# Storing the kept transposes of a two-layer banded kernel: the DMA issued by ScalarE in place of SyncE

## The chip, the cores and the metric

The kernel runs on one core of a Trainium2 chip. The core has a matrix engine (TensorE; PE in the profile, with its weight loads shown as PEld), a vector engine (VectorE, DVE), an activation engine (ScalarE, ACT), a general engine (GpSimd, POOL) and SyncE (SP), which here does nothing but issue DMAs. Each engine works through its own list of instructions in order and waits on semaphores for the others. The time is the device time of one execution in microseconds. An issue of a DMA stands in its engine's list like any other instruction; the transfer itself runs on 16 DMA engines.

## The reference

Two layers of the same form are applied to an image of 512 x 512 positions with 64 channels. In each, the input is normalised by groups of two channels over the whole image, then by channels at each position, and projected to 128 hidden channels five times (left, its gate, right, its gate, an output gate). The left values are read near the diagonal alone: output row i takes nine rows i-4 to i+4, each times one left value for the pair of rows and channel. The result is normalised over channels, gated, projected back and added to the input.

```
m, mask = src_mask, m[:, None] * m[None, :]
xn    = ln(group_norm(x))                          # 1 x 512 x 512 x 64
left  = (xn @ Wl + bl) * mask * sigmoid(xn @ Wlg + blg)
right = (xn @ Wr + br) * mask * sigmoid(xn @ Wrg + brg)
gate  = sigmoid(xn @ Wog + bog)
out[i, j, h] = sum over d in -4..4 of left[i+d, i, h] * right[i+d, j, h]
x     = x + (ln(out) * gate) @ Wo + bo             # and the same again with the second layer's weights
```

## The kernel before, in words

The rows are cut into nine overlapping blocks of 64 (`row_blocks`). The 128 partitions hold the 64 rows of a block twice: once for a column in the left half of the image and once for the column 256 further on. A chunk is 128 columns of each half, so there are 18 chunks a layer. A chunk is worked through in 16 units of eight columns (`Unit`, `NU`), 288 units a layer. One unit is one step of the loop in `layer` (line 846).

A unit passes these stages, several steps apart, so that in one step the engines work on different units:

- `load` (399) brings the unit's z from DRAM in two DMAs. GpSimd or VectorE applies the group norm (`scaled`, `moved`), VectorE takes statistics (`inner_stats`), GpSimd centres and rescales (`centred`, `rescaled`).
- `transposed` (452) turns z on TensorE into PSUM, and `kept` (471) copies the transposes to SBUF as the tile zT with ScalarE. zT has 192 columns for each of four column pairs: the first 128 are the transposes of both halves, written by a first activation of 128 x 512 elements; the last 64 repeat the first half, written by a second of 128 x 256. The pool `ztp` (1066) has two buffers for zT.
- zT serves `right` (516), eight products each for two halves of the unit, with `right_gate` (519, the sigmoid tile sg, on ScalarE) and `right_end` (523, the product into RO, on VectorE).
- The first 128 columns of zT are also stored in DRAM, in the tensor `later`, for the output gate, which is needed about 30 steps on (`LAG`, 787). `recall` (686) fetches them back as the tile zg two steps ahead of use; its pool `ztg` (1067) has two buffers. `gates` (690) projects zg on TensorE and `gated` (703) applies the sigmoid with ScalarE (the tile gate).
- `mix` (577) does the banded product with slabs A of the left values, which `take_left` (561) fetches from the DRAM tensor `left_of` in four DMAs each, eight slabs a chunk; ScalarE and VectorE copy the results back to RO ("copy a", "copy b").
- `norm` (675) writes the tile on, mostly by ScalarE, one or two of eight columns by GpSimd. `turned` (714) transposes it on TensorE, `times_gate` (727) makes ZH on VectorE, `end` (750) projects back, `ended` (763) adds the input (the tile XR, fetched by `fetch`, 739) and stores the output in two DMAs.

At the start of each layer some steps also make left values (`left`, 530), which are stored to `left_of` in groups of nine DMAs.

The order on each engine is written by hand. The lists `FIRST` and `SECOND` (38 to 54) name the stages of a step in order, for the first and the second layer; `InOrder` (373) keeps what is issued through `en` in the order of the program on its engine. A step starts with its DMAs (848 to 857): loads of z, the fetch of XR, slabs A, and zg. Then come the stages of the list; "keep" stands behind "transpose", and "end", with the output's stores, soon behind "keep". On ScalarE a step of the first layer runs, from "keep" on: two activations of zT, copies to RO, statistics in every fourth step, three of on, two of gate, two of sg, four of on.

A waiting instruction holds up all that stands behind it on its engine. All DMAs, whichever engine issues them, use eight semaphores in turn; each waits until the DMA eight places before it in the program's order has landed.

The helper that keeps the order records nearly every instruction at line 381, so the profile's rows are told apart by their tiles.

Of the kernel before, what the change touches and what calls it, by code (L numbers as in the profile page):

```python
# [16 lines left out]
P = 128  # L17
# [86 lines left out]
def tile_two_banded_layers(  # L104
# [366 lines left out]
    def kept(u: Unit):  # L471
        u.t = ztp.tile([P, JU // 2, P + S], F32, tag="zT", name="zT")
        to = u.t.rearrange("c k (n p) -> c n k p", n=3)
        for n, pt in enumerate(u.pt):
            en.scalar.activation(
                to[:, n : n + pt.shape[1]], pt.rearrange("c n (k p) -> c n k p", p=S),
                AF.Identity, bias=1.0,
            )
        if u.near is None:
            en.scalar.activation(  # L480
                to[:, 2], u.pt[0][:, 0].rearrange("c (k p) -> c k p", p=S), AF.Identity, bias=1.0
            )
            en.sync.dma_start(later[u.at], u.t[:, :, :P])

    def place(k: int, e: int) -> int:

# [297 lines left out]
    def layer(src: bass.AP, dst: bass.AP, w: dict, stats: bool, then=None):  # L784
# [61 lines left out]
        for t in range(min(loads), last_t + 3):  # L846
# [40 lines left out]
            for item in order:  # L887
# [41 lines left out]
                elif name == "keep":  # L929
                    for v in inputs(t + 1):  # L930
                        kept(v)
# [132 lines left out]
    later = dram.tile([len(blocks) * LH // JU, P, JU // 2, P], F32, name="later")  # L1064
# [45 lines left out]
```

## Time and profile before

| | |
|---|---|
| median of 3 runs | 4771.6 us (4764.16 to 4789.46) |
| the profiled execution | 4769.15 us |
| its span, first to last instruction | 4767.2 us |
| TensorE busy | 3885.2 us (81%) |
| weight loads busy | 3337.2 us (70%) |
| VectorE busy | 4007.1 us (84%) |
| ScalarE busy | 3608.6 us (76%) |
| GpSimd busy | 3274.7 us (69%) |
| granted TensorE clock, mean | 0.952 |
| DMA moved | 983.48 MB, 206 GB/s over the span |
| DMAs of `later` | 576 stores and 576 loads of 256 KB |

The busy shares are means over the whole span, of which about the first 270 us go to the statistics of the input and the setup, and a stretch near 2,450 to 2,650 us to the change from the first layer to the second. The layers' steady parts lie between. Issues of DMAs do not count as busy, so SyncE has no row in the table; its load is read from the rows of its issues (their queue is called SPq) and from its timeline. A wait's row says which engine waited before which tile, what ended the wait, the microseconds in total, how many times, and the longest.

### The profile page before, as it was taken

The page shows a single profiled execution, that of the slowest core. Times are in us where ns is not written, and L with a number is a line of the kernel's source. Part 1 is how long each engine was busy: PE and PEld are TensorE (multiplying, and loading weights), DVE is VectorE, ACT ScalarE, POOL GpSimd, SP SyncE. Part 2 cuts the span into 40 slices and gives each one's busy share as a digit, 9 for nine tenths or more (in the row PEclk, how much of TensorE's full clock was granted, in tenths as well). Part 3 has the DMA queues.
Part 4 walks back from the last instruction along what each step waited for, and adds up shares of the span by engine and source line. Part 5 has one row for each costly group of instructions (what it writes and reads, how often), then busy time and mean ns, then how long its engine had stood idle before and what let it go on. Part 6 is the DMA issues. An engine that isn't in the chain of part 4 may idle for free. (4 is left out here: it accounts for less than half of the span.)

```text
span 4767.2 us, 193179 instructions
## 1 busy us (share of the span) xinstructions
PE 3885.2 (81%) x76306; PEld 3337.2 (70%) x76306; DVE 4007.1 (84%) x10943; ACT 3608.6 (76%) x8410; POOL 3274.7 (69%) x3427
## 2 busy tenths in 40 slices
PE   1035899999999999999985478888888888888898
PEld 0024787888787878887864467777777777777776
DVE  7864888888888888888877488988899998999898
ACT  0023888888888888898974378888888888888887
POOL 0036888888888888888723487777777777777751
PEclk9987999999999999999997799999999999999999
DMA  7958677777777777777764867777777777777776
GB/s 311 401 120 126 182 208 204 212 217 211 212 208 208 210 208 209 214 212 210 207 171 110 104 189 208 214 220 208 210 221 214 221 212 211 213 219 215 217 200 185
DMA packets 1437809, 983.48 MB, mean 206 GB/s; under 512 B 167363, under 2 KB 1284585, under 8 KB 1432553
## 3 DMA queue, kind: packets, MB, share of 16 engines
q1 hardware_dynamic: 1432064, 969.69, 74.4%
q8 instruction: 604, 9.90, 0.9%
q14 instruction: 301, 2.46, 0.2%
q10 hardware_dynamic: 4840, 1.43, 0.1%
HBM read 658.35 MB, written 312.40 MB: 204 GB/s over the span
## 5 line engine op out<-in xcount | busy, mean ns | idle before, releaser
L381 ACT ACTIVATE on<-RO,nm,rs 128x128 f32<-128x128 f32 x3744 | 1588.5, 492 | 91.8 <-DVE nm L381 44.9
L381 PEld LDWEIGHTS banks<-pack,zT 64*128 64x128 f32 x18576 | 1304.4, 203 | 380.6 <-ACT zT L381 204.4
L381 PE MATMUL banks<-pack,zT 64*128 64x128 f32 x18576 | 1350.8, 292 | 174.4 <-ACT zT L381 149.3
L381 DVE TENSOR_TENSOR RO<-banks,sg 128x512 f32<-128x512 f32 (+1 forms) x1188 | 796.3, 677 | 464.4 <-ACT sg L381 387.6
L381 POOL TENSOR_SCALAR on<-RO,rs,nm 128x128 f32<-128x128 f32 x864 | 383.9, 451 | 975.7 <-ACT sg L381 504.5
L381 ACT ACTIVATE sg<-banks 128x512 f32<-128x512 f32 (+1 forms) x1188 | 695.0, 590 | 311.1 <-PE banks L381 287.1
L381 PE MATMUL bank<-zg,pack 64*128 64x448 f32 (+1 forms) x2304 | 727.3, 615 | 213.5 <-DMA zg<-later 193.8
L381 DVE BATCH_NORM_STATS2 sto<-RO 128x6 f32<-128x256 f32 x2304 | 803.8, 412 | 0.8
L381 DVE SCALAR_TENSOR_TENSOR ZH<-bank,pack,gate 128x448 f32<-128x448 f32 (+1 forms) x1152 | 739.5, 684 | 63.0 <-ACT gate L381 34.1
L381 ACT ACTIVATE gate<-bank 128x448 f32<-128x448 f32 (+1 forms) x1152 | 563.8, 541 | 172.6 <-issue 103.0
L381 POOL TENSOR_TENSOR z<-z,ga 128x512 f32<-128x512 f32 x536 | 681.2, 1279 | 17.2 <-DMA z<-mid_x 8.7
L381 PE MATMUL bank<-pack,ZH 128*64 128x64 f32 x18432 | 667.3, 226 | 17.8 <-DVE nm L381 16.7
L381 POOL TENSOR_TENSOR z<-z,gb 128x512 f32<-128x512 f32 x536 | 677.5, 1277 | 5.1
L381 POOL TENSOR_TENSOR z<-z,rs 128x512 f32<-128x512 f32 x586 | 618.3, 1056 | 71.6 <-DVE rs L381 44.6
L381 POOL TENSOR_TENSOR z<-z,sti 128x512 f32<-128x512 f32 x586 | 624.3, 1066 | 20.8 <-DVE sti L381 20.8
L381 PEld LDWEIGHTS bank<-pack,ZH 128*64 128x64 f32 x18432 | 587.4, 138 | 60.9 <-DVE nm L381 24.2
L381 ACT ACTIVATE zT<-banks 128x512 f32<-128x512 f32 (+1 forms) x1084 | 460.1, 475 | 72.0 <-PE banks L381 62.8
L381 DVE BATCH_NORM_STATS2 sti<-z 128x6 f32<-128x128 f32 x2344 | 504.1, 282 | 0.5 <-POOL z L381 0.3
L381 PE MATMUL bank<-ident,on 64*128 64x64 f32 x9216 | 453.8, 227 | 27.5 <-ACT gate L381 25.0
L381 PEld LDWEIGHTS bank<-zg,pack 64*128 64x128 f32 x2304 | 240.5, 191 | 336.5 <-DMA zg<-later 62.7
L381 PEld LDWEIGHTS bank<-ident,on 64*128 64x128 f32 x9216 | 426.5, 141 | 69.6 <-ACT gate L381 44.7
L381 DVE TENSOR_TENSOR XR<-bank,XR 120x512 f32<-120x512 f32 (+1 forms) x576 | 390.9, 679 | 2.5 <-PE bank L381 1.2
(154 smaller groups left out, 4020.5 us busy)
## 6 DMA issues: line engine op xcount, KB each, us to landing
later<-zT SPq DMA_DIRECT2D x576, 256.0 KB
A<-left_of SPq DMA_DIRECT2D x1152, 128.0 KB
zg<-later SPq DMA_DIRECT2D x576, 256.0 KB
z<-in_x_dram SPq DMA_DIRECT2D x576, 128.0 KB
z<-mid_x SPq DMA_DIRECT2D x576, 128.0 KB
gn_x<-in_x_dram SPq DMA_DIRECT2D x16, 4096.0 KB
XR<-in_x_dram SPq DMA_DIRECT2D x448, 112.0 KB
mid_x<-XR SPq DMA_DIRECT2D x448, 112.0 KB
```

Of the source, the lines that this page charges most:

```text
L381: return lambda *a, **k: tc.keep_in_program_order(f(*a, **k))
```

## The change

The store of a unit's transposes is issued by ScalarE; the data, the tiles and all else in the program stay.

```diff
     def kept(u: Unit):
         u.t = ztp.tile([P, JU // 2, P + S], F32, tag="zT", name="zT")
...
             en.scalar.activation(
                 to[:, 2], u.pt[0][:, 0].rearrange("c (k p) -> c k p", p=S), AF.Identity, bias=1.0
             )
-            en.sync.dma_start(later[u.at], u.t[:, :, :P])
+            en.scalar.dma_start(later[u.at], u.t[:, :, :P])
```

The store stays at its place in the program: directly behind the activations that write zT. On ScalarE the copies, on, gate and sg of the step now stand behind it; on SyncE the next DMA behind the fetch of zg is the store of the output.

## The prediction

> **What bounds the kernel now.** I read the windows first, to separate the two layers from their starts; then the waits; then SyncE's issues and its timeline beside ScalarE's. Busy time in two steady windows (columns: stretch, length, busy us and instructions per engine, granted clock, DMA share, GB/s):
>
> ```profile
> 700.00:2400.00 1700.00, 1583.57 (x32684) 1373.20 (x32677) 1466.60 (x3976) 1510.88 (x3537) 1396.24 (x1376) 0.98 0.76 210
> 2700.00:4600.00 1900.00, 1650.13 (x32720) 1439.55 (x32716) 1698.98 (x4623) 1558.24 (x3592) 1438.23 (x1586) 0.96 0.77 212
> ```
>
> Order: PE, PEld, DVE, ACT, POOL. In layer one PE is busy 93%, ACT 89%, DVE 86%; in layer two DVE 89%, PE 87%, ACT 82%. No compute engine is full, so something makes them wait for each other. The queue of DMA issues is not in these columns. Its rows (min/median/max ns):
>
> ```profile
> L381 SPq DMA_DIRECT2D later<-zT x576: 518/553/4745, 281.1 to 4622.3; - x192
> L381 SPq DMA_DIRECT2D A<-left_of x1152: 573/615/2165, 422.8 to 4666.2; - x192
> L381 SPq DMA_DIRECT2D zg<-later x576: 338/458/1883, 499.1 to 4755.4; - x192
> ```
>
> A step (one unit of eight column pairs; 288 a layer) issues on average one later, two A, one zg, two z (587), two XR in (462 or 481) and two XR out (480 or 506): 5.35 us by the medians, near 6.1 with 0.05 to 0.1 us between issues, and more with the tails. A step lasts 1700/231 = 7.4 us in layer one, 1900/268 = 7.1 in layer two, counting the evacuations zT in each window. SyncE is as full as PE, and its work comes in bursts. Its timeline (start, us, count) and what ScalarE and PE do meanwhile:
>
> ```profile
> 3000.49 1.06 SPq L381 DMA_DIRECT2D later<-zT  x1
> 3001.64 1.03 SPq L381 DMA_DIRECT2D out_dram<-XR  x2
> 3002.77 1.16 SPq L381 DMA_DIRECT2D z<-mid_x  x2
> 3003.99 1.02 SPq L381 DMA_DIRECT2D XR<-mid_x  x2
> 3005.11 3.62 SPq L381 DMA_DIRECT2D A<-left_of  x4
> 3008.83 0.55 SPq L381 DMA_DIRECT2D zg<-later  x1
> 3009.48 0.55 SPq L381 DMA_DIRECT2D later<-zT  x1
> ...
> 3014.08 0.56 SPq L381 DMA_DIRECT2D later<-zT  x1
> ```
> ```profile
> 3003.12 0.84 ACT L381 ACTIVATE zT<-banks 128x512 f32<-128x512 f32 x2
> 3003.86 0.89 ACT L381 ACTIVATE on<-RO,nm,rs 128x128 f32<-128x128 f32 x2
> ```
> ```profile
> 3012.12 1.87 PE L381 MATMUL bank<-zg,pack 64*128 64x448 f32 x4 [3.35 <-DMA zg<-later]
> ```
>
> From store to store SyncE needs 8.99 us in the step with A, 4.60 in the next without. The zT made at 3003.12 to 3003.96 is stored at 3009.48: SyncE is 5.5 us late. The zg issued at 3008.83 is read by PE at 3012.12, 3.29 us later, after PE idled 3.35. The waits in total (us, times, longest), the last two lines from the layer-one and the layer-two window:
>
> ```profile
> PE bank L381 <- DMA zg<-later: 193.8, 103, 6.9
> ACT zT L381 <- DMA later<-zT: 104.2, 13, 16.3
> SPq L381 <- ACT zT L381: 234.9, 122, 12.7
> DVE RO L381 <- ACT sg L381: 201.1, 267, 4.6
> DVE RO L381 <- ACT sg L381: 121.0, 83, 9.6
> ```
>
> So SyncE's lateness costs PE 194 us (zg) and ScalarE 104 us (a zT buffer still held by its late store). The second is at the starts of the layers, for instance:
>
> ```profile
> 341.81 14.34 SPq L381 DMA_DIRECT2D left_of<-RO  x9
> ...
> 366.91 0.66 ACT L381 ACTIVATE zT<-bank 128x256 f32<-128x256 f32 x2 [16.33 <-DMA later<-zT]
> ```
>
> **The change, part by part.** The built program moves 576 stores from SyncE to ScalarE, each behind the two activations that fill zT; PE, DVE and POOL keep their order, and no other DMA moves. Each store still waits for two things: the activation that fills the stored columns, and, as every DMA here does, the transfer eight places earlier in program order, whose semaphore it reuses.
>
> *Removed from SyncE.* One issue a step, 0.553 us by the median and some 0.1 between issues: 0.65 us a step, 11 steps of a burst giving back 7 us. The wait for zT goes too (234.9 us), but the stores of XR behind it wait for DVE at about the same place, so I count no gain for that. What was late next was zg. Its mean wait is 193.8/103 = 1.9 us, three stores' worth, so it should vanish from the third or fourth step of a burst on. I take two thirds: **-129 us**. Ends: 0 (SyncE stays late because a transfer, not the issue, sets it) and -194.
>
> *The held zT buffers.* At 341.81 nine stores of left_of keep SyncE for 14.34 us and zT's store waits behind them. From ScalarE it is issued without that queue, but its eighth predecessor is then often one of the nine, which must land. I take half of 104.2: **-50**; ends 0 and -104.
>
> *Added to ScalarE.* Without the store the instruction behind zT starts 0.74 us after zT's start (3003.12 to 3003.86). With it the first activation must end (0.58, the mean of 128x512 zT), then 0.04, the issue of 0.553, and 0.04 again (ScalarE's own issues at line 218 take 607 ns and start 648 apart): 1.21. The delay is 0.47; with the tail of the store's row (up to 4745 ns) I take 0.53, or 305 us for 576. The cover is ScalarE's idle time: (1700-1511)/231 = 0.82 us a step in layer one, (1900-1558)/268 = 1.27 in layer two. Behind the store in ScalarE's order stand the copies RO, the norms on, the two gates and the two sg; DVE's RO waits for sg, and frees banks for PE. sg ended a wait of DVE 267 times of 464 in the layer-one window and 83 of 542 in the layer-two window. So 0.53 x 288 x 0.58 = 88 us reach DVE in layer one and 0.53 x 288 x 0.15 = 23 in layer two. DVE is not the fullest engine of layer one and its RO is not always awaited; I take half: **+56**. Ends: 0 (ScalarE idle covers all) and +305 (cover gone).
>
> *The new wait.* ScalarE now waits at its store for a transfer that SyncE issues. No row shows this, so I take it from the step above: eight places before the store of 3009.48 stands the second z, issued about 3003.35, landing 3.29 us later, at 3006.6; zT ended at 3003.96, so ScalarE would have stood 2.6 us, with copies, gates and sg behind it. The freed 0.65 us a step shrinks the lateness, so I take one hold of 2 us in each of the 36 chunks (18 a layer, 16 steps each): **+72**. Ends: 0 (SyncE is never late) and 288 slab steps (1152/4) times 2.6, which is 749, if nothing shrinks and nothing covers.
>
> Sum on the profiled execution: 4767.2 - 129 - 50 + 56 + 72 = 4716, and 2 us outside the span (4769.15 against 4767.2) make **4718 us**. The profiled execution is 2 us under the median 4771.6, so no correction is needed.
>
> The Trainium skill speaks against this gain: in "DMA: Bandwidth & Descriptors", section "Issuing engines are not separate DMA queues", moving issues to another engine saves only the sequencer's time, usually small beside the transfer. Row: the issue is 0.55 us beside 3.29 to landing, small for one transfer, but ten a step fill SyncE. By the rule the sum is no change, 4769; by the rows it is 4718.
>
> The same page, section "Queues, rings and completion order", says that SyncE and ScalarE have no descriptor generator each of their own. In the trace, ScalarE's line-218 issues stay at 607 to 618 ns where one of SyncE's falls into them. If the rule meant that one waits out half of the other's issue, 0.27 us in 85% of 576 cases would be 132 us more on ScalarE.
>
> **The rivals.** (1) *ScalarE becomes the bound of layer one.* For it: 89% busy plus 0.53/7.4 is 96%. Against it: 0.82 us idle a step. Price: all of 0.53 x 288 = 153 there, 12 in layer two, no hold: 4769 - 129 - 50 + 165 = 4755, no change that a measurement tells (0.5%, 24 us). (2) *ScalarE is held by SyncE's transfers.* Place: its store in slab steps. For it: 5.5 us of lateness, where a step of this kind holds from about 2.8 on (6.1 us from the predecessor's issue to the store, less 3.29 to land). Against it: SyncE gains 0.65 us in each step. Price: 1.3 us (half of 2.6) in 288 steps, of which idle covers 0.8, is +144; zg gains only half (-65), and -50 and +56 stay: 4769 + 85 = 4854. It decides when SyncE's lateness in slab steps stays above 2.8 us. (3) *ScalarE's issue hides altogether and zg's wait ends:* 4769 - 194 - 50 + 28 = 4553. For it: idle time covers 0.53 in the mean step; against it: sg is awaited in most steps of layer one.
>
> **How the numbers follow.** Forecast 4718 (own range 4640 to 4745): 0.39; rival 3: 0.08; rival 1: 0.16; rival 2 and worse: 0.37. Faster by over 0.5% is 0.47, within it 0.16, slower 0.37. The range runs from 4630, between forecast and rival 3, to 4880, a little above rival 2: left out are about 0.08 below and 0.1 above.
>
> **What would show it.** PE's wait for zg well under 100 us; ScalarE's waits for later at the layer starts halved; ScalarE's gap behind zT near 0.5 us in most steps; waits of ScalarE's queue for z, XR or A in the hold, some 70 us. DVE's wait for sg should grow by under 100. Wrong would be: zg's wait unchanged (SyncE's issue was not the limit), ScalarE's store taking over 0.8 us, or holds of 2 us in most slab steps.

## The result, and the profile after

The changed kernel takes 4640.5 us (median of 4 runs, 4633.4 to 4643.1) against 4772.9 of the kernel before on the same chip: a ratio of 0.9729, 95% interval 0.9699 to 0.9759. The direction was forecast, with the time in the range; the size was not: 2.7% against the forecast 1.1%. The profiled execution has a span of 4641.2 us, 126.0 less than before; the sum of the prediction had 51 less.

The two windows of the changed kernel (second one 100 us shorter, since the kernel ends earlier; columns as before):

```profile
700.00:2400.00 1700.00, 1613.57 (x33373) 1384.28 (x33365) 1491.87 (x4038) 1529.45 (x3610) 1398.26 (x1382) 0.99 0.77 214
2700.00:4500.00 1800.00, 1632.40 (x32093) 1393.97 (x32093) 1674.88 (x4530) 1521.38 (x3570) 1388.06 (x1547) 0.98 0.80 219
```

In the first window each engine does more work in the same time: PE is busy 95% where it was 93%, DVE 88% (86%), ScalarE 90% (89%). In the second DVE has gone from 89 to 93%. The waits that the prediction spoke of, in the changed kernel's list (us, times, longest):

```profile
DVE RO L381 <- ACT sg L381: 248.3, 324, 4.3
...
PE bank L381 <- DMA zg<-later: 31.3, 21, 5.8
...
PEld bank L381 <- DMA zg<-later: 17.2, 13, 3.3
...
ACT zT L381 <- DMA later<-zT: 20.4, 6, 5.6
```

The rows of the kernel before that the prediction does not show, for the whole span as in the list above:

```profile
PEld bank L381 <- DMA zg<-later: 62.7, 28, 4.5
DVE RO L381 <- ACT sg L381: 387.6, 423, 9.6
SPq L381 <- DVE XR L381: 115.2, 80, 3.7
```

and SyncE's longest wait in the changed kernel:

```profile
SPq L381 <- DVE XR L381: 563.6, 309, 6.1
```

PE's wait for zg has fallen from 193.8 to 31.3 us. The weight loads have a row of their own for the same wait, which fell from 62.7 to 17.2. The two rows must not be added: laid over each other in time they cover 197.7 us before and 33.4 after, since 58.8 of the 62.7 us lie inside PE's idle time. DVE's wait for sg, which was to grow, fell from 387.6 to 248.3. SyncE no longer waits for zT and stands instead at the stores of XR, for DVE: 563.6 us where it was 115.2. It has time to spare.

The store's row, and ScalarE's timeline in a step where nothing is in the way and in one where something is (start, us):

```profile
L381 ACTq DMA_DIRECT2D later<-zT x576: 520/521/629, 282.0 to 4494.7; - x192
```
```profile
2924.46 0.87 ACT L381 ACTIVATE zT<-banks 128x512 f32<-128x512 f32 x2
2925.09 0.52 ACTq L381 DMA_DIRECT2D later<-zT  x1
2925.66 0.90 ACT L381 ACTIVATE on<-RO,nm,rs 128x128 f32<-128x128 f32 x2 [0.32 <-ACT zT L381]
```
```profile
2894.90 0.84 ACT L381 ACTIVATE zT<-banks 128x512 f32<-128x512 f32 x2
2897.86 0.52 ACTq L381 DMA_DIRECT2D later<-zT  x1
2898.42 0.58 ACT L381 COPY RO<-bank 128x512 f32<-128x512 f32 x1 [2.68 <-DMA XR<-mid_x]
```

In the first, on starts 1.20 us after zT where it started 0.74 after it before: the store delays ScalarE by 0.46 us. Of the 576 stores 454 overlap an issue of SyncE; their median is 521 ns, as that of the other 122, so the 132 us that the prediction priced in case one issue waits for the other do not occur. In the second the store stands from about 2895.5 to 2897.86 although its data is there: ScalarE waits for a transfer of SyncE's, eight places back. I measure this hold as the time from the end of the first zT activation to the issue, less the usual 0.05, where it is over 0.2. In two steady windows (700 to 2300 and 2750 to 4450 us) it comes to 81 us in 103 stores. By the order of the DMAs, the transfers eight places back were mostly fetches of XR (about 51 us) and loads of z (about 28 us).

To place the time, each execution is cut where VectorE begins the 61st and the last ZH of a layer (two a step, 576 a layer), which gives a start, a steady part of each layer and the change between the layers (us, read from the traces; the last 6 us are left out). The rows come from several chips, on which the median of the kernel before was 4757.7 to 4797.2 us. "After, load given back", "two issues for every other slab" and the last two runs below are from the slowest, so small differences from these mean little:

| profiled execution | start | layer one | change of layers | layer two |
|---|---|---|---|---|
| before | 737.6 | 1803.3 | 476.1 | 1744.2 |
| after | 718.0 | 1761.9 | 456.5 | 1698.9 |
| store left out | 692.9 | 1722.1 | 426.5 | 1639.8 |
| store left out, activation added | 695.1 | 1743.8 | 432.8 | 1649.6 |
| before, activation added | 726.7 | 1809.2 | 473.2 | 1767.3 |
| two issues a slab, store on SyncE | 718.2 | 1725.4 | 453.1 | 1643.6 |
| two issues a slab, store on ScalarE | 716.6 | 1748.5 | 444.4 | 1648.5 |
| after, load given back to SyncE | 744.8 | 1816.1 | 487.3 | 1756.3 |
| two issues for every other slab | 732.1 | 1749.9 | 470.3 | 1687.6 |

### The profile page after: what moved, and what is told of

It is laid out like the page before. It is cut to its first block, busy times and chain, and to the rows that moved or that the text cites. A ratio compares the mean times of both kernels' runs of the same rounds, so it can differ in the third digit from the quotient of the medians.

```text
span 4641.2 us, 192470 instructions
## 1 busy us (share of the span) xinstructions
PE 3888.9 (84%) x76306; PEld 3306.2 (71%) x76306; DVE 4003.3 (86%) x10943; ACT 3572.3 (77%) x8410; POOL 3274.0 (71%) x3427
## 5 line engine op out<-in xcount | busy, mean ns | idle before, releaser
L381 PEld LDWEIGHTS banks<-pack,zT 64*128 64x128 f32 x18576 | 1266.6, 196 | 358.0 <-ACT zT L381 131.4
L381 PE MATMUL banks<-pack,zT 64*128 64x128 f32 x18576 | 1332.7, 286 | 149.4 <-DVE RO L381 81.2
L381 DVE TENSOR_TENSOR RO<-banks,sg 128x512 f32<-128x512 f32 (+1 forms) x1188 | 786.8, 676 | 275.6 <-ACT sg L381 248.3
L381 ACT ACTIVATE sg<-banks 128x512 f32<-128x512 f32 (+1 forms) x1188 | 671.6, 591 | 219.3 <-PE banks L381 207.5
L381 PE MATMUL bank<-zg,pack 64*128 64x448 f32 (+1 forms) x2304 | 741.3, 602 | 90.0 <-ACT RO L381 38.0
L381 PEld LDWEIGHTS bank<-pack,ZH 128*64 128x64 f32 x18432 | 589.3, 139 | 62.7 <-DVE nm L381 25.1
L381 ACT ACTIVATE gate<-bank 128x448 f32<-128x448 f32 (+1 forms) x1152 | 561.2, 539 | 15.3 <-issue 7.9
L381 DVE BATCH_NORM_STATS2 sti<-z 128x6 f32<-128x128 f32 x2344 | 503.7, 282 | 17.3 <-POOL z L381 17.2
```

Source lines behind the costliest of these rows:

```text
L381: return lambda *a, **k: tc.keep_in_program_order(f(*a, **k))
```

## The experiments

**What freeing SyncE is worth with nothing on ScalarE.** The store is left out:

```diff
-            en.sync.dma_start(later[u.at], u.t[:, :, :P])
...
-        en.sync.dma_start(o.t, later[o.at])
+        en.sync.dma_start(
+            o.t, strided(x, o.at % (L * L * D // (P * JU // 2 * P)) * (P * JU // 2 * P),
+                         (JU // 2 * P, P), (P, JU // 2), (1, P)),
+        )
```

> Kernel before without the store of zT at all; zg is fetched from the input x instead (same size of fetch, other data). SyncE loses 576 issues and its wait for zT, ScalarE gets nothing, and 151 MB of writes are gone. Theory A (freeing SyncE is worth more than forecast, about the whole of the waits for zg and held zT, 250 us, and ScalarE's issue and hold cost about 120): 4500 to 4550 us. Theory B (freeing SyncE is worth the forecast 179 us, and ScalarE's costs are nearly hidden): 4580 to 4620 us. If the traffic of the stores matters by itself, it is below both.

Measured: ratio 0.9425 (0.9394 to 0.9455), 4490.6 us. That is somewhat below theory A's band. By the spans it is 280 us, where the prediction took 179 for SyncE freed and zT no longer held: 185 us in the steady parts and 94 at the starts of the layers (737.6 to 692.9, 476.1 to 426.5). The stores' writes are gone here too, and a time below both bands was to speak for them. The steady parts, 1722.1 and 1639.8, are within 4 us of the run with fewer slab issues below, where the writes remain, so there they are worth little. Whether they matter at the starts no run separates.

**The same with ScalarE's time, but no DMA.** In the place of the store:

```diff
+    idle = keep.tile([P, P], mybir.dt.bfloat16, name="idle")
...
+            en.scalar.activation(idle, all_ones, AF.Identity, bias=ln_eps, scale=ln_eps)
```

> As the run without the store, with one activation of 128x128 from constants to a scratch tile on ScalarE at the store's place (0.39 us from start to start, near the 0.45 us that the store delays ScalarE by). It has no DMA and no wait. Theory A: 60 to 80 us more than without it. Theory B: at most 20 us more.

Measured: 0.9506 (0.9469 to 0.9543), 40 us above the run without it, between the two theories. Of 576 x 0.39 = 225 us on ScalarE, idle time covers more than four fifths even when SyncE is out of the way.

**ScalarE's time in the kernel before.** The same line added behind the store that SyncE issues:

> Kernel before (store on SyncE) with the same extra activation of 0.39 us on ScalarE behind each zT. Charge of the prediction: +56 us scaled by 0.39/0.53, so 4815. If SyncE sets the pace of the kernel before, so that ScalarE's time is covered: within 20 us of 4773. If ScalarE's cover is gone: up to +225, 5000.

Measured: 1.0038 (1.0016 to 1.006), 18 us of the 225: mostly covered, as expected where SyncE sets the pace.

**Fewer issues on SyncE by another way.** The store stays where it was; a slab takes two issues:

```diff
-        for e in range(2):
-            for s in range(2):
-                en.sync.dma_start(
-                    A[e * S : (e + 1) * S, s * q : (s + 1) * q].rearrange("p h i t -> p h (i t)"),
...
+        for e in range(2):
+            en.sync.dma_start(
+                A[e * S : (e + 1) * S].rearrange("p (s h) i t -> p s h (i t)", s=2),
+                strided(
+                    left_of, n * size + h * q * span + 2 * WIN,
+                    (H // 2 * span, S), (H // 4 * span, 2), (span, q), (1, 2 * S),
+                ),
+            )
```

> Kernel before (store on SyncE) with the two halves of each slab half fetched in one DMA: two issues for A instead of four, 576 fewer in all, the same bytes, nothing on ScalarE. If SyncE's issue time is the limit, it gains at least what the change gains: 4560 to 4650 us (less if the larger issue takes longer than 0.62 us). If it is the store's place in the same queue or SyncE's wait for zT that matters, under 1%: 4730 to 4780.

Measured: 0.955 (0.9517 to 0.9583), 4549.1 us, better than the change. SyncE's row for A and the waits in this kernel:

```profile
L381 SPq DMA_DIRECT2D A<-left_of x576: 573/631/2077, 421.2 to 4443.6; - x192
```
```profile
ACT zT L381 <- DMA later<-zT: 98.0, 13, 16.0
...
PE bank L381 <- DMA zg<-later: 24.7, 23, 6.1
...
PEld bank L381 <- DMA zg<-later: 15.6, 13, 2.2
```
```profile
SPq L381 <- ACT zT L381: 345.6, 186, 12.7
```

Twice the bytes issue in 631 ns where half took 615: for these fetches SyncE's cost is by the issue, not by the byte. With 576 issues fewer PE's wait for zg falls from 193.8 to 24.7 us (with the weight loads' row laid over it, from 197.7 to 26.5), while the execution falls by 4.5%, some 212 us. The store is still in SyncE's queue, SyncE waits for zT longer than before (345.6 us against 234.9), and the store's 256 KB still go out from its queue: none of these was the limit of the steady parts. The count of issues was.

Fewer DMAs also use the eight semaphores less often, but that is not where the gain comes from: in the two windows of the kernel before, SyncE waited about 2 us in all for an earlier transfer to land.

**Both together.** The slab edit on the changed kernel:

> The changed kernel with two issues for each slab instead of four. SyncE is freed by 1152 issues. If SyncE's issues still limit the changed kernel in its slab steps: below 4600 us, and ScalarE's holds at the store go under 30 us. If PE, DVE and ScalarE set the pace by now: within 20 us of 4640.

Measured: 0.9602 (0.9585 to 0.962), 4570.0 us: SyncE still limited the changed kernel. The holds at the store shrink to 12 us in 22 stores (81 in 103). But it is no better than the kernel with the store on SyncE, by the profiled spans 4564.0 against 4546.4: once SyncE has few issues, the move to ScalarE costs more than it brings.

**Half the dose.** The two-issue form for odd slabs only:

> Kernel before with two issues for every other slab and four for the rest: 288 issues fewer. If the time goes with SyncE's issues one for one: half of 212 us, 4655. If half is enough to end most waits for zg: 4560 to 4620. If nothing is gained until SyncE keeps up: above 4700.

Measured: 0.9683 (0.9652 to 0.9714), 3.2% of the 4.5% for half of the issues. The times are from different chips (before: 4797.2 here), so the ratios are compared: on the chip of the other run this one is 4610 us, in the second band. Half of the issues bring over two thirds of the gain, although only half of the wait for zg is gone (PE's row is at 102.6 us, 106.4 with that of the weight loads laid over it).

**Giving SyncE its issue back.** First attempt, a DMA of 64 single elements, from a constant and from zT, and the same on ScalarE without the store:

```diff
+    junk = dram.tile([len(blocks) * LH // JU, S, 1], F32, name="junk")
...
             en.scalar.dma_start(later[u.at], u.t[:, :, :P])
+            en.sync.dma_start(junk[u.at], all_ones[:S, :1])
```

> The changed kernel; SyncE issues at the old place of the store a DMA of 64 elements from a constant to DRAM (0.59 us of issue, 256 bytes, no wait for zT). If SyncE's issue time is what the change saved: 4740 to 4800 us. If it was the wait for zT or the 256 KB in SyncE's queue: 4630 to 4670.

> As the run before, but the 64 elements are read from zT, so SyncE waits for ScalarE's activation as before the change, and zT's buffer is held until this DMA has landed. If the issue time is all: within 20 us of the run with the constant. If the wait and the held buffers count too: 30 to 100 us above it.

> Without the store (zg from x), and ScalarE issues at the store's place a DMA of 64 elements from a constant (0.6 us of issue, with the wait for the transfer eight places earlier). Against the run with the plain activation it adds the hold and 0.2 us of issue. Theory A: 40 to 80 us above that run. Theory B: under 20 us above. Against the changed kernel it lacks only the stores' traffic: within 20 us of 4640 if traffic does not matter.

Measured: 1.3998 (1.395 to 1.4046), 1.4093 (1.4044 to 1.4141) and 1.2915 (1.2887 to 1.2942). None of these answers its question, since the tiny writes hold up most other transfers. SyncE's waits in the first of them:

```profile
SPq L381 <- DMA junk<-all_ones: 1175.5, 329, 6.0
SPq L381 <- DMA later<-zT: 212.8, 86, 9.1
SPq L381 <- DVE XR L381: 157.4, 89, 5.2
```

So the wait for zT by SyncE was tried alone in no usable run. Second attempt, a load of 16 KB:

```diff
+    idle = keep.tile([P, D], F32, name="idle")
...
             en.scalar.dma_start(later[u.at], u.t[:, :, :P])
+            en.sync.dma_start(idle[:S], x[u.blk.s : u.blk.s + S, u.j, :])
```

> The changed kernel; SyncE issues at the old place of the store a load of 64 rows of 256 bytes from x to a scratch tile (16 KB, no wait for zT). The two runs with 256 bytes written in 4-byte pieces doubled the landing times of their neighbours, so they do not answer this. If SyncE's issue time is what the change saved: the gain is gone and ScalarE's costs stay, 4760 to 4880 us. If it was the wait for zT or the store's 256 KB in SyncE's queue: 4630 to 4670.

Measured: 1.0046 (1.0026 to 1.0065), 4818.8 us: the whole gain is gone and a little more. But PE's wait for zg has not come back. The waits, the load's row, and a store in this kernel:

```profile
ACT zT L381 <- DMA later<-zT: 27.7, 6, 8.6
...
PE bank L381 <- DMA zg<-later: 18.4, 17, 6.3
```
```profile
L381 SPq DMA_DIRECT2D idle<-in_x_dram x576: 465/485/2587, 269.4 to 4662.2; - x192
```
```profile
3122.32 0.84 ACT L381 ACTIVATE zT<-banks 128x512 f32<-128x512 f32 x2
3125.94 0.54 ACTq L381 DMA_DIRECT2D later<-zT  x1
```

ScalarE stands at its store for 3 us in this step, and by the measure above 210 us in 188 stores. SyncE is late again: its issues fill 78 and 82% of the two steady parts, against 71 and 78% in the changed kernel and 81 and 83% in the kernel before. The lateness now seems to be paid at ScalarE's store, which feels it before zg does: against the changed kernel the holds grow by 129 us. One DMA more in each step also shifts which transfer stands eight places back: the held stores here stood mostly behind fetches of XR (about 162 us). How much of the longer hold comes from that shift and how much from the lateness is not separated.

**The issue and the hold without the store's traffic.** The load of the last run, issued by ScalarE, with the store left out:

> Without the store (zg from x); ScalarE issues at the store's place the 16 KB load of 64 rows from x, with its wait for the transfer eight places earlier. It has ScalarE's issue and hold without the store's traffic and without held zT buffers. Extra activation alone cost 40 us over 4491. If the hold costs about its length (81 us in the changed kernel): 4570 to 4620 us. If the hold is covered by ScalarE's idle time: 4520 to 4550.

Measured: 0.9507 (0.948 to 0.9533), 39 us by the ratio above the run with nothing on ScalarE. This run is not what it was meant to be: the load does not read zT, so its issue runs beside the activation and in three quarters of the steps starts more than 0.5 us before that ends. Its steady parts are within 8 us of those of the run without it (1730.0 and 1639.1 against 1722.1 and 1639.8), although on this chip the kernel before is 36 us slower; the starts are 62 us longer (722.4 and 459.2 against 692.9 and 426.5). So the loss is at the starts, and the 35 us of holds in the steady windows cost little. What a hold of the changed kernel costs this run does not settle.

**A version that takes the best of both.** Two issues a slab, and the store on ScalarE in the first 16 units of a layer alone:

```diff
-            en.sync.dma_start(later[u.at], u.t[:, :, :P])
+            queue = en.scalar if u.at < NU else en.sync
+            queue.dma_start(later[u.at], u.t[:, :, :P])
```

> Two issues for each slab; the store goes to ScalarE only in the first 16 units of each layer, where SyncE is held by the stores of left_of, and stays on SyncE in the other 272. If held zT buffers at the layer starts cost what the waits say (98 us in the run with two issues, of which the changed kernel lost 80 but showed 20 of time): 10 to 40 us less than 4549. If the starts are set by the transfers of left_of themselves: within 10 us of 4549.

Measured: 0.9492 (0.9458 to 0.9526). The interval overlaps that of the slab edit alone (0.9517 to 0.9583), so no gain is shown. ScalarE's wait for held zT falls from 98.0 to 23.5 us, yet start and change of layers are not shorter (727.6 and 460.1 us against 718.2 and 453.1, on the slower chip). The best of the kernels that keep the store are these two, about 4.5 and 5% under the kernel before.

## Why the prediction was wrong in size

By the table of parts, with the runs to tell the terms apart:

| step | forecast | shown | by which comparison |
|---|---|---|---|
| SyncE freed, steady parts | -129 | -179 | two issues a slab against before: 1803.3 to 1725.4, 1744.2 to 1643.6 |
| held zT, or whatever sets the starts | -50 | -39 | after against before: start and change |
| ScalarE's issue | +56 | +28 | steady parts, store on ScalarE against SyncE, both with two issues a slab |
| the new wait (hold) | +72 | +64 | steady parts, after against the same with two issues a slab |
| sum | -51 | -126 | spans 4767.2 and 4641.2 |

The shares rest on one profiled execution of each kernel, on several chips, and the first line takes it that 576 fewer slab issues free SyncE as much as 576 moved stores. The steady lines lead from one kernel to the next (before, two issues a slab, the same with the store on ScalarE, after), so they add up to the measured change by construction; what they show is the split. Another way through the runs gives nearly the same: store left out -185, activation added +32, from there to the changed kernel +67. The line of the hold is what the other 576 slab issues cost with the store on ScalarE, so it may hold more of SyncE's lateness than the hold alone.

**The step that failed** is the first term of the sum, "I take two thirds: -129 us". The mechanism was right, the size was not: freeing SyncE measured 179 to 185 us in the steady parts, near the term's end of -194. The discount of a third, for the first steps of a burst, was not borne out: of PE's 193.8 us for zg, 162.5 went in the changed kernel and 169.1 with two issues a slab. The weight loads' row, 62.7 us, adds next to nothing to it, since it lies almost wholly inside PE's. The remaining 10 to 20 us of the gain are outside PE's wait for zg; where they come from is open. Of the 75 us between the forecast sum and the measured one, this term makes up 50 and the next one 28.

**ScalarE's issue** was read rightly as a delay (0.47 forecast, 0.46 seen), but charged double. I took DVE's waits for sg as proof that ScalarE's delay passes on to DVE. Much of sg's lateness itself came from SyncE: DVE's wait for sg, 387.6 us before, fell when SyncE was freed, to 191.3 us with the store left out and 200.1 with two issues a slab. That it came through zg, PE and the gates is likely but not isolated; ScalarE's idle time before the gate went with it, from 172.6 to 15.3 us in the groups of the two pages (before, then after):

```profile
L381 ACT ACTIVATE gate<-bank 128x448 f32<-128x448 f32 (+1 forms) x1152 | 563.8, 541 | 172.6 <-issue 103.0
L381 ACT ACTIVATE gate<-bank 128x448 f32<-128x448 f32 (+1 forms) x1152 | 561.2, 539 | 15.3 <-issue 7.9
```

**Held zT:** the wait went (104.2 to 20.4), and the starts gained 39 us, but not for the reason given, so that this term came near is luck. With two issues a slab the wait stays at 98.0, and the starts gain as much, 42 us. That wait was not what set the starts. What did, beyond the issues of SyncE, is not settled; only leaving the store out altogether gained more.

**The new wait** came out near its size, 72 forecast, 81 us of standing, 64 us in the sum, but by luck: not 36 holds of 2 us but 103 of 0.8 us in the two windows alone. Rival 2 had its mechanism right: where SyncE does not gain the issue, as with the load given back, the hold grows to 210 us in the steady windows and the gain is gone. It lost because most stores were not held: 103 of some 470. Rival 1, ScalarE as the bound of layer one, did not happen: layer one gained 41 us. Rival 3 went too far the other way.

**The rule of the Trainium skill** that moving issues between engines saves only their sequencer's time ("DMA: Bandwidth & Descriptors", "Issuing engines are not separate DMA queues") holds here in its first half, as far as the runs tell: with one short issue a step given back to SyncE, but neither the wait for zT nor the 256 KB, the gain is gone. "Usually small relative to the DMA itself" is true of one transfer (0.55 us against 3.3 to landing) and misleads here: ten issues of half a microsecond in a step of seven were the limit, and 576 of them are worth 4.5%.

## What to carry to other kernels

Count the issues of a DMA queue in a step and multiply by the row's duration: a queue that issues has no busy share in the profile, and it can be as full as the busiest engine. Here its issues filled 81 and 83% of the two steady parts, 90 and 92% with the gaps of at most 0.15 us between them. Cut the number of issues first, by putting two transfers in one, before moving an issue to an engine that computes: there it delays all that stands behind it, and it may wait for the other queue's transfers as well. When a wait for one transfer is priced, look at the rows of all engines that wait for it, but lay them over each other in time before adding any: two rows can be the same idle time seen twice. Then ask whether other waits in the list are its echo.

## What was not expected of the hardware

A store of 64 elements of 4 bytes, 256 bytes in all, once a step, made the kernel 40% slower when SyncE issued it and 29% without the large store when ScalarE did. The issue is short (476 ns median), but the transfer lands after about 8.4 us (median from issue to the last update of its semaphore), and loads of z that landed in 3.3 us now take 7.4. The page of the run on SyncE has the same bytes at a lower rate, 147 GB/s against 206 before:

```profile
DMA packets 1483889, 983.67 MB, mean 147 GB/s; under 512 B 213442, under 2 KB 1330664, under 8 KB 1478632
```

The fetches of A and zg, which are issued last before the next tiny write, landed about as before (3.7 and 3.8 us). A load of 64 rows of 256 bytes at the same place landed in about 3.5 us and did nothing of the kind. Why the tiny writes hold up the others was not tried.
